# Layer 3's chunk norm in the output projection's place and one step earlier, and one state more for the producers in layer 1's finish and feed

## The chip, the core and the metric

The kernel runs on one core of a Trainium2 chip, as one program of four layers with the image data kept in HBM between them. The metric is the device time of one execution in microseconds; the runs shown are compared by their median. All arithmetic is float32. The engines are named as in the profile: PE (TensorE matmul), DVE (VectorE), ACT (ScalarE), POOL (GpSimd), and SP, which issues nearly all DMAs.

## The reference

Layers 1 and 3 are what the change touches. Both contain Mamba blocks, whose core is a scan over tokens for each of 16 states:

```
def step(h, inp):                       # layer 3; layer 1 is the same with other names
    dt_t, B_t, C_t, x_t = inp
    dA = jnp.exp(dt_t[:, :, None] * A)
    h = h * dA + (dt_t * x_t)[:, :, None] * B_t[:, None, :]
    y = jnp.einsum('bdn,bn->bd', h, C_t)
    return (h, y)
...
def rms_norm(x, w):
    return x * lax.rsqrt(jnp.mean(x * x, axis=-1, keepdims=True) + EPS) * w
def mamba1(x, ...):
    xn = rms_norm(x, nw)                # this is the "chunk's norm"
    ...                                 # projections, causal conv, scan, gate
    return y @ opw.T
...
xt = mamba_bidir(xt, P, 0, 1) @ tlin_w + tlin_b + xt    # "output projection" with the residual
xf = mamba_bidir(xf, P, 2, 3) @ flin_w + flin_b + xf
```

Layer 1, over 8 images of 64 x 64 pixels and 64 channels, scans in four directions, and then does, per image, a layer norm over 128 channels, a gate `y * silu(z)`, an output projection, a second norm, and a feed-forward part: a 1x1 and a depthwise 3x3 convolution, `gelu(h1) * h2`, and a 1x1 convolution.

## The kernel before, in words

**The scan stream.** `stream` (L462) drives layers 1 and 3. Work comes in steps of 1024 tokens-times-channels columns, and each step has 16 states, numbered n = 0 to 15 here; "3/8" will mean state 8 of step 3. A state i goes through a fixed pipeline: SP loads the rows of B and C (`fetch`), POOL or PE makes `hb` (the product with B: L526 on POOL, or `expand`, L2207, eight pieces of a product on PE, at states 1, 2, 5, 6, 9 and 10 of layer 3), ACT makes `dA` by an exponential (L520), DVE scans (L550), DVE or POOL multiplies by C (L564; POOL for the "shared" states), and PE adds the result up in PSUM (L310, L320). Every engine takes its instructions in the order in which the program issues them, so an instruction that waits holds up all that is queued behind it on its engine. The order is written by hand: nothing is reordered later.

**Tasks beside the scan.** All other work is cut into generators, "tasks", which are advanced by a piece at a time. `advance` (L437) is called once per state, before that state's scan is issued, and runs one piece. A piece ends at a `yield`: `yield True` means that the task holds the one PSUM buffer `mm` across the cut ("held"; the same task goes on until it lets go), `yield False` means that the next piece needs no PSUM, a bare `yield` means that the next piece wants PSUM and needs a "room". So a `yield` costs no instruction: it puts the following instructions one state later in the engines' queues.

**Layer 3.** It runs twice (s = 0, 1) over 16 chunks c of 2048 tokens: 32 chunks. A chunk has 8 steps (4 groups g of 512 tokens, forward and backward, k = 0, 1), so 128 states. Three things interleave with the scans:
- `prepare` of the step after next, by the fixed table `plan` (projection L2130, softplus, the six small diagonal DMAs `place` L2125 at states 3, 4, 5, 8, 9, 11, the gate).
- `begin`, the norm of the next chunk: eight DMAs `raw<-x` (L2044, 128 KB each, in pieces of 256 bytes); for each half j of the chunk a Square on ACT (L2053), the mean over channels on PE into `mm` (L310, `mm<-sq,mean`), a copy on ACT (L2058), a DMA to `rs` (L2060); then Sqrt (L2063), reciprocal on DVE (L2066), a DMA to HBM (L2069), eight broadcast DMAs `inv<-rs` (L2076, 256-byte pieces as well), and four multiplications `xn<-raw,inv` on POOL (L2083), `9` states apart.
- `finish`, the output projection of a group (L2246, L2249 on PE into `mm`, L2265 on ACT), which the end of every second step puts into the queue `urgent`.

`Step.rooms` names the states at which a piece that wants PSUM may run, `lets` the state at which a held `mm` is let go (ACT reads it, just before the scan of that state). Before the change, rooms are 7 and 11; `urgent` goes first and takes only 11; while `urgent` has a task that waits for its room, `behind` (the norm) does not move at all. `begin` of chunk c+1 is queued at the end of the first step of chunk c. `expand` of state 10 takes `mm` at state 7, after first releasing whatever holds it. `ready` forces the whole of a norm out before the first `prepare` that needs it (step 6, state 13).

**Layer 1.** Eight images, each 16 steps (4 directions, 4 pieces), so 256 states an image. While image b is scanned, the tasks of the image before run: `finish` (four times: POOL multiplies `inv` by z, L1162; PE applies `cent1`; DVE multiplies, L1167; projections; ACT copy), `begin` of image b+1, and `feed` (four times: three groups of convolution on PE; gelu on ACT, L1230; DVE multiplies, L1233; gelu, L1241; DVE multiplies, L1244). At state 2 of every step `begin_next` (inside `stream`) must hand `mm` to `prepare`, so it advances a held task until that task lets go, however many pieces that takes.

Of the kernel before, what the change touches and what calls it, by code (L numbers as in the profile page):

```python
# [16 lines left out]
NB = 8  # L17
# [255 lines left out]
class Net:  # L273
# [163 lines left out]
    def advance(self, behind, room=True, calm=True):  # L437


        while True:  # L440
            queue = self.held or (self.urgent if self.urgent else behind)
            if not queue or not (room or queue[0].said is False):
                return
            task = queue[0]
            if task.calm and not calm:
                return
            task.step()
            self.held = queue if task.said is True else None
            if not task.over:
                return  # L450
            queue.popleft()
# [10 lines left out]
    def stream(self, pools, ahead, steps, behind, rest=None):  # L462
# [115 lines left out]
        begun = {}  # L578
# [17 lines left out]
        for i in range(total + 2):  # L596
            at, n = divmod(i, NS)
            need(i + ahead[0], "bc")
            need(i + ahead[1], "du")
            fetch_c(i + ahead[2])  # L600
            fetch(i + ahead[0])
            multiply_b(i + ahead[1])
            if 0 < i <= total and shared(i - 1):
                multiply_c(i - 1)


            def begin_next():
                more = at + (2 if plan else 1)
                if more < len(steps) and n == steps[at].start:
                    steps[more].ready()  # L610
                    while self.held or self.urgent and not plan:
                        self.advance(behind)
                    return Task(steps[more].prepare())
                return work

            first = i > NS and n == 2
            if plan:
                before, behind_scan = plan.get(n, (0, 0))
                for _ in range(before if work else 0):
                    work.step()  # L620
                work = None if work and work.over else work
                if 2 < i <= total + 2 and shared(i - 3):
                    gather(i - 3)
                if 1 < i and not first and not shared(i - 2):
                    gather(i - 2)
                self.advance(behind, n in steps[0].rooms and not (n == 7 and self.urgent))
                if n in steps[0].lets and self.held:
                    self.release()
                if i < total:
                    scan(i)  # L630
                work = begin_next()
                for _ in range(behind_scan if work else 0):
                    work.step()
                if first:
                    gather(i - 2)
                if i < total and not shared(i):
                    multiply_c(i)
                if not direct(i + 2):
                    decay(i + 2)
                elif lent(i + 2):  # L640
                    expand(i + 2)
                if direct(i + 3):
                    decay(i + 3)
                    if not lent(i + 3):
                        expand(i + 3)
                continue
            late = i > 1 and not first and steps[0].late and shared(i - 2)
            if i > 1 and not late and not first:
                gather(i - 2)
            work = begin_next()  # L650
            if work is not None and not (self.held and work.said is None) and (calm(i) or not work.calm):
                work.step()
                if work.over:
                    work = None
            room = work is None or work.said is not True and (n < steps[0].early or hasattr(steps[at + 1], "du"))
            self.advance(behind, room, calm(i))
            if late:
                gather(i - 2)
            if i < total:
                scan(i)  # L660
            if first:
                gather(i - 2)
            if i < total:
                if not shared(i):
                    multiply_c(i)
            decay(i + 2)
# [292 lines left out]
    def layer1(self, src, dst):  # L959
        nc, tc, d = self.nc, self.tc, self.d  # L960
        mid = self.hbm["x1a"]
        with ExitStack() as ctx:
# [176 lines left out]
            def finish(b, chunks=range(4)):  # L1139

                q, rows = b // 2, slice((b % 2) * C, (b % 2) * C + C)
                hold = images[b]
                y = hold["y"]
                sums, again = hold.setdefault("sums", {}), hold.setdefault("again", {})

                def centred(c):
                    ps = pp.tile([128, T], F32, name="mm")
                    self.mm(ps, cent1, y[:, c * T : c * T + T])
                    yield True
                    return ps  # L1150

                yield from statistics(sums, centred, False, self.eps5, chunks)

                def output(c):
                    at = slice(c * T, c * T + T)
                    inv = spread(sums, c)
                    z = tp.tile([128, T], F32, name="tmp")
                    nc.sync.dma_start(z, hz[b, :, at])
                    x = tokens(src, b, c)
                    yield False  # L1160
                    yield
                    nc.gpsimd.tensor_tensor(inv, inv, z, ALU.mult)  # L1162
                    ps = pp.tile([128, T], F32, name="mm")
                    self.mm(ps, cent1, y[:, at])
                    yield True
                    yield True
                    nc.vector.tensor_tensor(inv, ps, inv, ALU.mult)  # L1167
                    yield
                    ps = pp.tile([128, T], F32, name="mm")
                    self.mm(ps, w_bias, z, start=True, stop=False)  # L1170
                    yield True
                    self.mm(ps, w_out, inv, start=False, stop=False)
                    self.sides(ps, self.ident2, x, start=False)
                    yield True
                    yield True
                    x = tp.tile([128, T], F32, name="tmp")
                    nc.scalar.copy(x, ps)
                    nc.scalar.dma_start(mid[q, rows, at], x[:C])
                    yield
                    ps = pp.tile([128, T], F32, name="mm")  # L1180
                    for r in range(2):
                        side, o = slice(r * C, r * C + C), slice(r * 512, r * 512 + 512)
                        nc.tensor.matmul(ps[:, o], centd[side], x[side, o], start=True, stop=True)
                    yield True
                    return ps

                yield from statistics(again, output, True, self.eps6, chunks)

            def feed(b, part=None):
# [37 lines left out]
                def gated(c):  # L1227
# [2 lines left out]
                    nc.scalar.activation(g, ps, AF.Gelu)  # L1230
                    yield
                    ps = yield from group(c, slice(128, 256))
                    nc.vector.tensor_tensor(g, ps, g, ALU.mult)  # L1233
                    yield
                    x = tokens(mid, b, c)
# [3 lines left out]
                    if c < 2 and part is None:  # L1239
                        fetch(c + 2)  # L1240
                    nc.scalar.activation(h, ps[:106], AF.Gelu)  # L1241
                    yield True
                    yield True
                    nc.vector.tensor_tensor(h[:42], ps[C : C + 42], h[:42], ALU.mult)  # L1244
# [36 lines left out]
            behind = deque()  # L1281
# [634 lines left out]
    def layer3(self, src, dst):  # L1916
# [8 lines left out]
        with ExitStack() as ctx:  # L1925
# [108 lines left out]
            def begin(s, c):  # L2034
# [5 lines left out]
                from_ = srcs[s][q, rows, part * 4 * W : (part + 1) * 4 * W].rearrange("p (s t) -> p s t", t=HW)  # L2040
                for g in range(4):
                    at = slice(g * H, g * H + H)
                    for r in range(2):
                        nc.sync.dma_start(x[r * C : r * C + C, at, ends[r]], from_[:, at])  # L2044
                        yield False
# [35 lines left out]
                for g in range(4):  # L2081
                    at = slice(g * H, g * H + H)
                    nc.gpsimd.tensor_tensor(hold["xn"][:, at], x[:, at], inv[:, at], ALU.mult)  # L2083

                    for _ in range(9 if g < 3 else 1):
                        yield False

            behind = deque()
            begun = {}
            images = {}  # L2090

            class Step:
                bc_shape, start = [128, 2, W], 13
                direct, lent, rooms, lets = fed, (1, 5, 9), (7, 11), (13,)
                plan = {
                    2: (0, 1), 3: (2, 0), 4: (1, 0), 5: (1, 0), 6: (0, 1), 7: (1, 0), 8: (1, 0), 9: (1, 0), 10: (0, 1), 11: (1, 0), 13: (0, 1), 15: (1, 0)
                }
# [132 lines left out]
                def done(self):  # L2230
                    hold = chunks[self.s, self.c]
                    if self.k == 1:
                        net.urgent.append(Task(finish(self.s, self.c, self.g, [hold["y0"], hold["y1"]])))
                    more = self.s * 2 * NB + self.c + 1
                    if self.k == 0 and self.g == 0 and more < 4 * NB:
                        at = divmod(more, 2 * NB)
                        begun[at] = Task(begin(*at))
                        behind.append(begun[at])

            def finish(s, c, g, ys):  # L2240
                w, dst = weights[s], dsts[s]
# [28 lines left out]
            with tc.manual_schedule():  # L2270
# [7 lines left out]
                steps = [  # L2278
                    Step(s, c, g, k) for s in range(2) for c in range(2 * NB) for g in range(4) for k in range(2)
                ]  # L2280
                self.stream(pools, (6, 3, 6), steps, behind)


# [24 lines left out]
```

## Time and profile before

| what | us |
|---|---|
| median of 3 runs (23713.9 to 23741.58) | 23733.38 |
| the profiled execution, device time | 23722.93 |
| its span, first to last instruction | 23721.1 |

The span by stage, from the trace's windows (busy us of each engine):

| stretch of the span, us | stage | length | PE | DVE | ACT | POOL | DMA share |
|---|---|---|---|---|---|---|---|
| 0 to 967 | layer 0, first norm of layer 1 | 967 | 739.14 | 448.44 | 459.95 | 57.76 | 0.34 |
| 967 to 8350 | layer 1 | 7383 | 6261.24 | 6673.97 | 3939.50 | 6781.89 | 0.89 |
| 8350 to 11247 | last feed-forward of layer 1, layer 2 | 2897 | 2452.07 | 2396.48 | 1370.19 | 2246.55 | 0.65 |
| 11247 to 23721 | layer 3 | 12474 | 10813.17 | 11850.59 | 9165.00 | 11492.05 | 0.62 |

Columns from PE on are busy time; an engine that is busy for nearly the whole length of a stretch bounds it. The mean granted clock of TensorE is 0.933. A row of the timeline, as shown in the prediction, reads: start, duration, engine, line, operation, tiles, how many instructions were merged, and in brackets the idle time of the engine before it with what ended the wait.

### The profile page before, as it was taken

Reading aid. Unit: us, or ns where it says so; the run is one execution under the profiler, and the core shown is the slowest. Engines: PE = TensorE matmul, PEld = TensorE weight load, DVE = VectorE, ACT = ScalarE, POOL = GpSimd, SP = SyncE. Lnnn points to the kernel's source line nnn. Section 1 sums busy time; section 2 is a strip of 40 time slices with the busy share of each in tenths; the row PEclk is TensorE's granted clock in tenths of the full one; section 3 lists DMA queues with packets and bytes.
Section 4 is the critical chain, followed back from the end, with each engine's and each line's share of the span. In section 5 each row is a group of like instructions: output and inputs, shape, how many; then the busy total and the mean of one; then the engine's idle time right before and its main releaser. Section 6 shows DMA issues by size and latency. Waiting matters only on the chain. (4 is left out here: it accounts for less than half of the span.)

```text
span 23721.1 us, 288888 instructions
## 1 busy us (share of the span) xinstructions
PE 20265.6 (85%) x99226; PEld 9428.8 (40%) x99226; DVE 21369.5 (90%) x12265; ACT 14934.6 (63%) x19503; POOL 20578.3 (87%) x9876
## 2 busy tenths in 40 slices
PE   7778888888888888879888888888888888888888
PEld 5323333333333323322444444444444444444444
DVE  5599999999999859977899999999999999999999
ACT  5445555555555446632677777777777777777776
POOL 0499999999999849986899999999999999999998
PEclk9889999999999999999899999999999999999999
DMA  3599889898898849961566666666666666666665
GB/s 80 190 325 322 309 313 320 312 318 317 310 317 312 287 148 340 342 212 35 171 184 185 179 183 184 182 183 182 184 183 184 183 185 183 184 181 184 182 182 172
DMA packets 2857344, 5295.40 MB, mean 223 GB/s; under 512 B 1357208, under 2 KB 1363452, under 8 KB 2853568
## 3 DMA queue, kind: packets, MB, share of 16 engines
q1 hardware_dynamic: 2831296, 5213.58, 68.9%
q10 hardware_dynamic: 24576, 63.33, 0.7%
q8 instruction: 785, 12.86, 0.2%
q14 instruction: 687, 5.63, 0.1%
HBM read 5112.98 MB, written 162.40 MB: 222 GB/s over the span
## 5 line engine op out<-in xcount | busy, mean ns | idle before, releaser
L526 POOL TENSOR_TENSOR hb<-du,bc 128x1024 f32<-128x1024 f32 x3072 | 7222.3, 2363 | 665.9 <-DVE h L550 301.5
L550 DVE TENSOR_TENSOR_SCAN dA<-dA,hb 128x1024 f32<-128x1024 f32 x2488 | 5675.5, 2281 | 189.4 <-POOL hb L526 105.7
L526 POOL TENSOR_TENSOR hb<-du,b 128x1024 f32<-128x1024 f32 x2048 | 4877.0, 2410 | 468.6 <-DVE dA L550 215.7
L564 POOL TENSOR_TENSOR h<-h,bc 128x1024 f32<-128x1024 f32 x2208 | 5175.8, 2359 | 106.1 <-DVE h L550 90.9
L520 ACT ACTIVATE dA<-dt,w_A 128x512 f32<-128x512 f32 x5120 | 3522.2, 689 | 1483.8 <-DVE hc L564 706.8
L520 ACT ACTIVATE dA<-dt,w_l_A 128x1024 f32<-128x1024 f32 x2560 | 2857.3, 1117 | 1006.1 <-DVE hc L564 765.3
L310 PE MATMUL acc<-hc,ident 128*128 128x512 f32 x7040 | 3387.3, 618 | 89.2 <-DVE img L1367 48.0
L550 DVE TENSOR_TENSOR_SCAN dA<-dA,carry,hb 128x1024 f32<-128x1024 f32 x1320 | 3093.1, 2343 | 120.9 <-POOL hb L526 59.0
L564 DVE TENSOR_TENSOR hc<-dA,bc 128x1024 f32<-128x1024 f32 x2400 | 2937.8, 1224 | 141.4 <-issue 2.7
L310 PE MATMUL acc<-h,ident 128*128 128x512 f32 x3200 | 1865.3, 712 | 880.4 <-POOL h L564 855.3
L320 PE MATMUL acc<-h,ident 64*64 64x512 f32 x16384 | 2156.7, 626 | 459.5 <-POOL h L564 458.7
L2207 PE MATMUL dA<-bc,duT 128*128 128x128 f32 x12288 | 1862.7, 314 | 546.6 <-ACT z L2183 518.3
L310 PEld LDWEIGHTS acc<-hc,ident 128*128 128x128 f32 x7040 | 1397.0, 202 | 2091.4 <-issue 1726.8
L2207 PEld LDWEIGHTS dA<-bc,duT 128*128 128x128 f32 x12288 | 1704.1, 222 | 1176.8 <-ACT z L2183 696.4
L320 PE MATMUL acc<-hc,ident 64*64 64x512 f32 x16384 | 2108.2, 608 | 0.0
L520 ACT ACTIVATE hb<-dt,w_A 128x512 f32<-128x512 f32 x3072 | 2038.7, 711 | 9.9
L550 DVE TENSOR_TENSOR_SCAN h<-hb,mm 128x1024 f32<-128x1024 f32 x768 | 1741.6, 2268 | 219.6 <-PE acc L320 179.0
L550 DVE TENSOR_TENSOR_SCAN h<-hb,dA 128x1024 f32<-128x1024 f32 x768 | 1752.0, 2281 | 189.4 <-PE dA L2207 157.3
L564 DVE TENSOR_TENSOR hc<-dA,c 128x1024 f32<-128x1024 f32 x1408 | 1722.7, 1224 | 118.1 <-DMA c<-bc 5.7
L550 DVE TENSOR_TENSOR_SCAN h<-dA,hb 128x1024 f32<-128x1024 f32 x712 | 1622.7, 2279 | 27.3 <-ACT dA L520 26.4
L2207 PE MATMUL mm<-bc,duT 128*128 128x128 f32 x12288 | 1603.8, 287 | 1.4 <-ACT u L2141 1.4
L2207 PEld LDWEIGHTS mm<-bc,duT 128*128 128x128 f32 x12288 | 1556.8, 205 | 3.3 <-ACT u L2141 2.2
(336 smaller groups left out, 26794.5 us busy)
## 6 DMA issues: line engine op xcount, KB each, us to landing
bc<-bc SPq DMA_DIRECT2D x2560, 512.0 KB
b<-bc SPq DMA_DIRECT2D x2048, 512.0 KB
c<-bc SPq DMA_DIRECT2D x2048, 512.0 KB
bc<-bc SPq DMA_DIRECT2D x512, 1024.0 KB
bc<-dg SPq DMA_DIRECT2D x1536, 256.0 KB
bc<-bc SPq DMA_DIRECT2D x1536, 256.0 KB
tmp<-rs SPq DMA_DIRECT2D x93, 512.0 KB
raw<-x SPq DMA_DIRECT2D x256, 128.0 KB
```

The costliest lines, as they stand in the source:

```text
L310: self.nc.tensor.matmul(o, lhsT, r, start=start, stop=stop)
L320: self.nc.tensor.matmul(acc[j * C : j * C + C, r * 512 : r * 512 + 512], lhsT(j)[at, at], rhs[at, j * 512 : j * 512 + 512], start=start, s ...
L520: nc.scalar.activation(o[:, cut], s.dt[:, cut], AF.Exp, scale=A[:, n : n + 1])
L526: nc.gpsimd.tensor_tensor(s.shaped(hb[i]), s.shaped(s.du), B.pop(i), ALU.mult)
L550: nc.vector.tensor_tensor_scan(h[:, way], dA[i][:, way], b[:, way], s.first(n), ALU.mult, ALU.add)
L564: engine.tensor_tensor(s.shaped(o), s.shaped(h), CC.pop(i), ALU.mult)
L2207: nc.tensor.matmul(hb[:, at], self.duT[:, at], diag[:, m * 128 : m * 128 + 128], start=True, stop=True)
```

## The change

In layer 3 `rooms` becomes the single state 11 (the norm's PSUM pieces take the place in a step that the output projection has), the norm of chunk c+2 is queued at the end of chunk c's last step (one step before the old place), a norm's pieces without PSUM may run while `urgent` waits for its room, the load of a chunk's last quarter waits until the old chunk's projection has been issued, and the four multiplications by `inv` stand 6 states apart. In layer 1 three `yield`s are added: after the POOL multiplication L1162, before the DVE multiplication L1233, and before the DVE multiplication L1244. No instruction is added or removed.

```diff
@@ advance
-            queue = self.held or (self.urgent if self.urgent else behind)
+            queue = self.held or self.urgent or behind
+            if not self.held and self.urgent and behind and not room and self.urgent[0].said is not False and behind[0].said is False:
+                queue = behind
@@ stream
-                self.advance(behind, n in steps[0].rooms and not (n == 7 and self.urgent))
+                self.advance(behind, n in steps[0].rooms)
@@ layer 1, finish
                     nc.gpsimd.tensor_tensor(inv, inv, z, ALU.mult)
+                    yield
                     ps = pp.tile([128, T], F32, name="mm")
@@ layer 1, feed
                     ps = yield from group(c, slice(128, 256))
+                    yield True
                     nc.vector.tensor_tensor(g, ps, g, ALU.mult)
...
                     nc.scalar.activation(h, ps[:106], AF.Gelu)
+                    yield True
                     yield True
                     yield True
                     nc.vector.tensor_tensor(h[:42], ps[C : C + 42], h[:42], ALU.mult)
@@ layer 3, begin
                 for g in range(4):
                     at = slice(g * H, g * H + H)
+                    while g == 3 and net.urgent:
+                        yield False
...
-                    for _ in range(9 if g < 3 else 1):
+                    for _ in range(6 if g < 3 else 1):
                         yield False
@@ layer 3
+            def start(s, c):
+                begun[s, c] = Task(begin(s, c))
+                begun[s, c].said = False
+                behind.append(begun[s, c])
...
-                direct, lent, rooms, lets = fed, (1, 5, 9), (7, 11), (13,)
+                direct, lent, rooms, lets = fed, (1, 5, 9), (11,), (13,)
@@ layer 3, Step.done
-                    more = self.s * 2 * NB + self.c + 1
-                    if self.k == 0 and self.g == 0 and more < 4 * NB:
-                        at = divmod(more, 2 * NB)
-                        begun[at] = Task(begin(*at))
-                        behind.append(begun[at])
+                    more = self.s * 2 * NB + self.c + 2
+                    if self.k == 1 and self.g == 3 and more < 4 * NB:
+                        start(*divmod(more, 2 * NB))
@@ before the stream of layer 3
+                start(0, 1)
                 self.stream(pools, (6, 3, 6), steps, behind)
```

## The prediction

> **What bounds it now.** I read the page's busy line, then its slices, then the windows by stage. The change touches layers 1 and 3 only.
>
> ```profile
> PE 20265.6 (85%) x99226; PEld 9428.8 (40%) x99226; DVE 21369.5 (90%) x12265; ACT 14934.6 (63%) x19503; POOL 20578.3 (87%) x9876
> DVE  5599999999999859977899999999999999999999
> POOL 0499999999999849986899999999999999999998
> ```
>
> In layer 3 DVE is busy 11850.59 of 12474 us, POOL 11492.05. The starts of DVE's scans (L550) in the timeline give every state's length. A step has 16 scans of 2.28 us, 8 products of 1.22 and a drain of 1.2: in the timeline they follow each other with no gap over most of a step, and an undisturbed step takes 47.5 us. The mean of the 31 chunks that carry a norm is 387.1 us, against 8 x 47.5 = 380: some 7 us a chunk, 218 us in all, is what better placing can reach. By step (0 to 7) the means are 48.2, 47.5, 47.9, 49.9, 49.6, 47.8, 48.8, 47.5. In layer 1 an image takes 917 us, POOL is busy 849 of them and DVE 836: POOL leads, DVE is close.
>
> **Layer 3, step 3: the norm's first half.** The timeline of the sixth chunk, states 8 to 10:
>
> ```profile
> 13430.88 2.62 PE L310 MATMUL mm<-sq,mean 64*1 64x512 f32 x4 [1.72 <-ACT z L2183]
> 13433.43 3.78 PE L2207 MATMUL dA<-bc,duT 128*128 128x128 f32 x16
> 13433.59 1.00 ACT L2058 COPY sq<-mm 1x1024 f32<-1x1024 f32 x1
> 13434.61 0.52 SPq L2060 DMA_DIRECT2D rs<-sq  x1
> 13437.32 2.29 DVE L550 TENSOR_TENSOR_SCAN h<-hb,dA 128x1024 f32<-128x1024 f32 x1 [2.39 <-PE dA L2207]
> 13437.39 1.08 ACT L2053 ACTIVATE sq<-raw 64x1024 f32<-64x1024 f32 x1 [2.80 <-DMA rs<-sq]
> 13440.95 2.29 DVE L550 TENSOR_TENSOR_SCAN h<-hb,mm 128x1024 f32<-128x1024 f32 x1 [1.35 <-PE acc L320]
> ```
>
> The mean's products stand on PE in front of the expansions for states 9 and 10, so DVE waits 2.39; the next Square stands on ACT behind a DMA just issued. States 8 and 9 together last 9.04 us here, and 6.67 in the mean of the other steps. The change moves the products to state 11 of step 1, the copy to 13. The second half does exactly this in step 3 now, and states 11 to 15 of step 3 show no loss. So 2.37 x 31 = **-74 us**. What is late next is the usual wait at state 9 (0.6 to 1 us in every step), which stays. The second Square now stands in step 1, state 15, behind its DMA: by the same DMA of step 3 (issued 1.9 us into state 15; 2.8 us to landing) it has landed before ACT gets there. Its 1.07 us push the exponentials for state 2, which now end 1.2 us before their scan: +0.1 us a chunk at most. The first Square goes from 2/0 to 1/1, the same phase, and cost nothing there.
>
> **Layer 3, steps 5 to 7: the four multiplications (1.40 us each) on POOL.** Now the first goes out at 5/12 and the rest at once at 6/13, forced by `ready`:
>
> ```profile
> 14376.32 4.13 POOL L2083 TENSOR_TENSOR xn<-raw,inv 128x560 f32<-128x560 f32 x3
> ...
> 14417.59 1.99 PE L320 MATMUL acc<-h,ident 64*64 64x512 f32 x8 [3.52 <-POOL h L564]
> ...
> 14429.12 2.29 DVE L550 TENSOR_TENSOR_SCAN h<-hb,dA 128x1024 f32<-128x1024 f32 x1 [0.98 <-ACT hb L520]
> ```
>
> POOL has 2.6 us to spare in a step (47.5 less 10 + 8 products of 2.36 and one of 2.4), so 4.13 at once leave it late through all of step 7: PE waits for L564, then the expansion for state 1 is late (the row names ACT, which had long been done; PE's expansion ended 0.1 us before). States 0 and 1 last 6.55 us in step 0, 7.16 in step 6, and 5.77 in quiet steps: 0.78 and 1.39 us. By the built order the four now go to 5/4, 5/10, 6/0 and 6/6. At 5/4, 6/0 and 6/6 POOL's own gaps follow (0.7, 0.8, 0.6 at states 2 to 4; 0.2 and 1.15 at 8 and 9) and take them up. At 5/10 none follows until state 2: everything for the next step is 1.4 us late. Here a rule speaks against the change: the Trainium skill ("TensorE: Matmul & The Clock Gate", section "Why this matters for your kernels") wants no idle gap of PE over about 3 us, lest its clock fall by half. PE's gap there is about 1.3 us; 1.3 + 1.4 = 2.7 stays under the rule: slack 0.8 us, cost 0.6 x 31 = 19 us. The row says less room: in the trace groups after gaps of 2.5 us and more often run at half speed (1.99 against 1.09 us above), and the seven chunks whose step 7 is late by 1.35 to 1.6 us lose 0.87. I take the row: 27 us. So step 6 gains (1.39 - 0.87) x 31 = **-16**, and step 0 (0.78 less the 0.15 that step 1, also without PE work at 11, loses now) x 31 = **-20**.
>
> **Layer 3, SP.** An issue takes 0.6 us alone, and up to 6.8 where one of the six `place` DMAs falls into the same state:
>
> ```profile
> L2044 SPq DMA_DIRECT2D raw<-x x256: 585/635/5205, 11247.1 to 23027.4; - x128
> L2076 SPq DMA_DIRECT2D inv<-rs x256: 579/1962/6824, 11279.6 to 23213.8; - x128
> ```
>
> (minimum/median/maximum ns.) Behind them the loads of B and C wait, then POOL. `inv` moves from 5/2..5/9, with five `place`, to 4/7..4/10 and 4/14..5/1, with two: better, and the phase in which `raw` stands now at no visible loss. `raw` takes the bad phase, 0/3 to 0/8, with four. In step 5 that delayed POOL by 0.95 us in the mean, 3.1 at worst; beyond 0.9 it reaches DVE, which gives 0.43 us by the same chunks. Ends: 0 and 1.3; I take 0.4 x 31 = **+12**. Step 2's loss of 0.15, from `raw` at 1/7, goes: -4; step 5 and the second Square give +3. The row DMA moves from 4/14 to 4/3, where SP has no backlog: nothing. Sqrt and reciprocal stay at 4/0 to 4/2, with their 2.3 us. Layer 3: -74 - 16 - 20 + 12 - 4 + 3 = **-99 us**.
>
> **Layer 1.** What the yields are to remove, in images 2 to 7 (1837 to 7340 us), from the waits:
>
> ```profile
> DVE tmp L1244 <- ACT tmp L1241: 64.0, 12, 5.4
> DVE tmp L1233 <- PE mm L1025: 62.7, 24, 6.2
> DVE tmp L1167 <- POOL tmp L1162: 32.9, 21, 2.9
> ```
>
> Twelve waits of 5.4 us, and six of the 24 with 6.2, are at state 2 of a step, where `begin_next` runs a held task to its end; another `yield True` there only lengthens that loop. The rest, about 59 us, is DVE waiting while POOL is busy or itself waits for a DMA (L1162 <- hz: 13.4 us): the time between such a wait and the next POOL product shows POOL idle only at 2/2, 2/3, 14/0 and 14/2. I count 2.8 us an image, not 10.
>
> Against it: shifted by a state here and there, pieces fall under the loop of state 2. Stepping through both orders, it runs 13 pieces an image now and 26 afterwards (four of them empty). The price, from two drains of the fourth image:
>
> ```profile
> 4252.18 2.83 PE L1025 MATMUL mm<-strip,hright 64*106 64x512 f32 x12
> 4255.05 1.02 ACT L1241 ACTIVATE tmp<-mm 106x1024 f32<-106x1024 f32 x1 [1.70 <-PE mm L1025]
> 4256.11 1.23 DVE L1244 TENSOR_TENSOR tmp<-mm,tmp 42x1024 f32<-42x1024 f32 x1 [5.30 <-ACT tmp L1241]
> ...
> 4317.86 1.23 DVE L1233 TENSOR_TENSOR tmp<-mm,tmp 128x1024 f32<-128x1024 f32 x1 [6.21 <-PE mm L1025]
> ```
>
> At 10/2 and 13/2 the convolution's right taps, until now issued a state earlier, join the drain. The drain at 11/2 already has them and waits 6.21 without the gelu; with the gelu's 1.02 and its hops that is 7.5 against 5.3: +2.2 each, 4.4. At 5/2 three quarters of the statistics of `begin` come at once: a chain of three copies and two Squares on ACT (1.0 each) and four PE groups (1.0 to 1.1) is about 11 us in front of an exponential; DVE has some 6 us of work meanwhile (scans, products, the drain L1367) and POOL one product more in hand: +3. At 3/2 and 4/2 projections join: +1.3. At 6/2 and 12/2: +0.8. Sum 9.5 - 2.8 = 6.7 an image, x6 = 40; the last image, with 24 drained pieces for 15, +6. Layer 1: **+46 us**, between 0 and 225 (below).
>
> **The sum.** The profiled execution took 23722.9 us: 23722.9 - 99 + 46 = 23670. The median of the runs is 10.4 higher; halving that, I predict **23675 us**.
>
> **Rivals.**
> - *Layer 1 is free*: POOL's buffers cover the longer drains, as they cover part of the present ones (DVE waits 6.2, POOL 4 to 5). 23733 - 99 = 23634, or some 20 lower if the step-0 loads cost nothing. Against it: POOL is already empty at 10/2 and 13/2. Chance 0.20.
> - *Layer 3 gives half back*: every chunk's `raw` in step 0 behaves like the worst `inv` chunks of step 5 (2 us late at DVE): +50 more, so -49 + 46: 23730. For it: the phase is the same. Against it: four collisions, not five, and the output projection keeps PE busy at 0/11. Chance 0.18.
> - *Slower*: each drained piece costs what one costs now. Around the drains of layer 1 POOL idles some 33 us an image for 13 pieces, 2.5 us each. 13 more: 33 x 6 + 25 = 225 against 99: 23733 + 126 = 23859. It decides from 1.1 us a piece on (87 pieces against 99 us). Against it: the empty pieces and the last piece of a chain cost nothing. Chance 0.13.
> - That the change doesn't do what it says is excluded by the built order.
>
> **The numbers.** Forecast 0.49, its own range 23625 to 23720. A measurement here tells 0.2%, 47 us, from no change. Faster by more: 0.34 of the forecast and the 0.20 of free drains, 0.54. Same: 0.15 of the forecast, 0.16 of the half-back case, 0.31. Slower: 0.15. The range from 23590 to 23760 leaves out the slower rival and the tail of the free one.
>
> **What would show it.** States 8 and 9 of step 3 as in other steps, no `rs<-sq` wait before L2053 (70.7 us in 29 now); states 0 and 1: about 5.9 us in step 0, 6.6 in step 6, 6.2 in step 1; `inv` issues mostly at 0.6 us; the wait of L1167 gone while the image stays at 917 us or grows to 924. It would be wrong if layer 3's chunks don't come down to about 384 us, or if an image of layer 1 moves by over 10 us.

## The result, and the profile after

| what | before | after |
|---|---|---|
| median of 20 runs each, us | 23717.79 (23706.0 to 23745.29) | 23757.04 (23733.22 to 23784.75) |
| ratio of after to before, 95% interval | | 1.0016, [1.0009, 1.0023] |
| span of the profiled execution, us | 23721.1 | 23744.8 |

The change makes the kernel slower, by about 39 us. Forecast was 23675, faster by over 0.2% as the likeliest case; 23757 is at the upper edge of the stated range, on the wrong side of before. The sign is clear of noise, the size is just under 0.2%.

The page of after, busy time and slices:

```profile
PE 20169.9 (85%) x99226; PEld 9371.3 (39%) x99226; DVE 21371.1 (90%) x12265; ACT 14940.4 (63%) x19503; POOL 20575.2 (87%) x9876
...
DVE  5598988988989949988799999999999999999999
...
POOL 0499989999999939986799999999999999999999
```

The instruction counts are those of before and so is the busy time of DVE and POOL, within some 3 us: all of the difference is waiting. The slices show where most of it lies: in the first half, where layer 1 is, digits of DVE have fallen from 9 to 8; in the second half, layer 3, they show next to nothing. The starts of DVE's scans give it in us. (State n of step k, written k/n, is here the time from that scan's start to the next. Lines of kernel.py are shifted by a few from kernel to kernel: the scan is L550 before and L552 after.)

| from the starts of the scans, us | before | after | difference |
|---|---|---|---|
| layer 1, 2048 scans | 7754.7 | 7828.5 | +73.8 |
| an image of it (mean of images 1 to 6) | 917.2 | 929.6 | +12.4 |
| layer 3, first to last scan | 12379.9 | 12333.8 | -46.1 |
| a chunk of it (mean of 31) | 387.06 | 385.66 | -1.40 |

The forecast had +46 for layer 1 and -99 for layer 3. Both signs are right and both sizes are wrong, and each error goes the same way. By step (0 to 7), the chunks of layer 3 moved by -5, +11, **+31**, -69, -35, +13, **+9** and +1 us in all (mean difference by 31), where the forecast had -8 for step 0, 0, -4, -74, 0, +3, -16 and 0.

### The profile page after: what moved, and what is told of

Read it like the earlier page. It is cut to its first block, busy times and chain, and to the rows that moved or that the text cites. A ratio compares the mean times of both kernels' runs of the same rounds, so it can differ in the third digit from the quotient of the medians.

```text
span 23744.8 us, 289011 instructions
## 1 busy us (share of the span) xinstructions
PE 20169.9 (85%) x99226; PEld 9371.3 (39%) x99226; DVE 21371.1 (90%) x12265; ACT 14940.4 (63%) x19503; POOL 20575.2 (87%) x9876
## 5 line engine op out<-in xcount | busy, mean ns | idle before, releaser
L552 DVE TENSOR_TENSOR_SCAN dA<-dA,hb 128x1024 f32<-128x1024 f32 x2488 | 5675.6, 2281 | 185.0 <-POOL hb L528 116.8
L566 POOL TENSOR_TENSOR h<-h,bc 128x1024 f32<-128x1024 f32 x2208 | 5179.3, 2360 | 110.8 <-DVE h L552 105.6
L522 ACT ACTIVATE dA<-dt,w_A 128x512 f32<-128x512 f32 x5120 | 3521.3, 689 | 1515.4 <-DVE hc L566 718.8
L522 ACT ACTIVATE dA<-dt,w_l_A 128x1024 f32<-128x1024 f32 x2560 | 2857.4, 1117 | 1007.7 <-DVE hc L566 760.7
L552 DVE TENSOR_TENSOR_SCAN dA<-dA,carry,hb 128x1024 f32<-128x1024 f32 x1320 | 3094.2, 2344 | 148.0 <-POOL hb L528 79.6
L566 DVE TENSOR_TENSOR hc<-dA,bc 128x1024 f32<-128x1024 f32 x2400 | 2937.8, 1224 | 141.0 <-issue 2.7
L522 ACT ACTIVATE hb<-dt,w_A 128x512 f32<-128x512 f32 x3072 | 2039.1, 711 | 10.7
L552 DVE TENSOR_TENSOR_SCAN h<-hb,mm 128x1024 f32<-128x1024 f32 x768 | 1742.1, 2268 | 214.6 <-PE acc L320 151.1
L552 DVE TENSOR_TENSOR_SCAN h<-hb,dA 128x1024 f32<-128x1024 f32 x768 | 1752.2, 2281 | 135.7 <-PE dA L2219 73.5
L566 DVE TENSOR_TENSOR hc<-dA,c 128x1024 f32<-128x1024 f32 x1408 | 1722.8, 1224 | 124.8 <-DMA c<-bc 12.2
L552 DVE TENSOR_TENSOR_SCAN h<-dA,hb 128x1024 f32<-128x1024 f32 x712 | 1622.7, 2279 | 47.2 <-ACT dA L522 40.0
L566 POOL TENSOR_TENSOR h<-h,c 128x1024 f32<-128x1024 f32 x640 | 1518.4, 2373 | 19.4 <-ACT carry L1355 19.0
```

The source lines that it names most:

```text
L522: nc.scalar.activation(o[:, cut], s.dt[:, cut], AF.Exp, scale=A[:, n : n + 1])
L552: nc.vector.tensor_tensor_scan(h[:, way], dA[i][:, way], b[:, way], s.first(n), ALU.mult, ALU.add)
L566: engine.tensor_tensor(s.shaped(o), s.shaped(h), CC.pop(i), ALU.mult)
```

## Where the time went, in the trace of after

**Layer 1, from the scan of 5/2 to that of 5/4.** It took 9.6 us an image before and takes 24.7 now. The timeline of after, fourth image:

```profile
3985.73 1.02 PE L1052 MATMUL mm<-tmp,mean 64*1 64x512 f32 x4
3986.80 1.00 ACT L1057 COPY tmp<-mm 1x1024 f32<-1x1024 f32 x1 [0.72 <-PE mm L1052]
...
3990.13 1.54 PE L1052 MATMUL mm<-tmp,mean 64*1 64x512 f32 x4 [1.15 <-ACT tmp L1047]
...
3995.99 1.87 PE L1052 MATMUL mm<-tmp,mean 64*1 64x512 f32 x4 [1.15 <-ACT tmp L1047]
3997.91 1.00 ACT L1057 COPY tmp<-mm 1x1024 f32<-1x1024 f32 x1 [1.97 <-PE mm L1052]
...
3998.97 3.68 PE L310 MATMUL mm<-u,w_l_xp 128*68 128x512 f32 x4 [1.10 <-ACT tmp L1057]
...
3999.68 1.12 ACT L522 ACTIVATE dA<-dt,w_l_A 128x1024 f32<-128x1024 f32 x1
...
4004.12 1.28 ACT L1062 ACT_TABLE_LOAD   x1 [0.43 <-ACT dbl L1329]
...
4005.77 0.35 DVE L1064 RECIPROCAL rs<-rs 128x32 f32<-128x32 f32 x1 [12.89 <-ACT carry L1355]
...
4006.03 2.25 DVE L552 TENSOR_TENSOR_SCAN h<-dA,carry,hb 128x1024 f32<-128x1024 f32 x1
```

The drain (the pieces that `begin_next` forces out at state 2 of a step) runs the norm's statistics as one chain, PE, ACT, PE, ACT, each link waiting for the one before. It begins with the copy at 3986.80, and the exponential (L522) stands behind it at 3999.68, 12.9 us later. But that is not what DVE waits for last. The exponential ends at 4000.80, and the scan starts at 4006.03: it stands behind the norm's reciprocal, which waits for the Sqrt (L1062; the row blames the `carry` copy that precedes it on ACT), which stands on ACT behind the copy of a projection that took PE 3.68 us. DVE sits idle for 12.89 us, POOL for 14.27.

**Layer 3, 2/0 and 2/1: the second Square.** The timeline of after, fifth chunk (`SPq` rows are issues):

```profile
13028.62 1.00 ACT L2065 COPY sq<-mm 1x1024 f32<-1x1024 f32 x1
...
13030.05 0.37 SPq L2232 DMA_DIRECT2D bc<-bc  x1
...
13033.73 4.66 POOL L566 TENSOR_TENSOR h<-h,bc 128x1024 f32<-128x1024 f32 x2
...
13036.11 0.32 SPq L2232 DMA_DIRECT2D bc<-bc  x1
13036.53 0.54 SPq L2067 DMA_DIRECT2D rs<-sq  x1
...
13040.61 1.08 ACT L2060 ACTIVATE sq<-raw 64x1024 f32<-64x1024 f32 x1 [2.38 <-DMA rs<-sq]
...
13042.99 1.33 ACT L522 ACTIVATE hb<-dt,w_A 128x512 f32<-128x512 f32 x2
...
13044.41 2.29 DVE L552 TENSOR_TENSOR_SCAN h<-hb,mm 128x1024 f32<-128x1024 f32 x1 [1.95 <-ACT hb L522]
```

The copy ends at 13029.62, but its row DMA is issued at 13036.53. Ahead of it on SP stand two loads of B and C (L2232). Each is issued in under 0.4 us, but the second waits 5.6 us for the first of the two POOL multiplications (L566). Such a wait stands in state 15 of step 3 too, before and after: it is the order of the program, and no slowness of the load. The row DMA lands 4.1 us after its issue. ACT comes to the Square 2.38 us before that, and the exponential for the next state, queued behind, makes DVE wait 1.95. This chunk is one of the worse ones. In the median of 30 chunks the row DMA goes out 2.5 us after the scan of 1/15; where the Square waits for it (26 times) it takes 3.6 us to land in the median, and the least is 3.1. The waits of layer 3, before and after:

```profile
DVE h L550 <- PE dA L2207: 157.3, 189, 2.7
...
DVE h L550 <- ACT hb L520: 23.9, 14, 4.8
```

```profile
DVE h L552 <- ACT hb L522: 79.2, 53, 4.0
DVE h L552 <- PE dA L2219: 73.5, 163, 2.1
...
ACT sq L2060 <- DMA rs<-sq: 29.1, 26, 2.9
```

(total us, times, longest.) By the scan that waits, the 84 us that DVE no longer waits for PE's expansions are mostly three things: 3/9 (63.6 before, 4.4 now) and 4/5 (27.7, 6.7), which are most of the gain of steps 3 and 4, and 6/1, where the wait only has another name: 24.3 for PE and 11.1 for ACT before, 49.7 for ACT (26 times) in after. The second Square's own share of the 79.2 is the wait at 2/2, 20.3 us in 22 times, where before had none. The Square's wait for its DMA fell from 70.7 us to 29.1, and did not go.

## Experiments

Each is compared with runs of the kernel before on the same chip.

**The two parts apart.** First the change of layer 3 alone, that is after without layer 1's three yields:

```diff
-                    yield            # behind L1164, z
-                    yield True       # ahead of L1237
-                    yield True       # ahead of L1249
```

> The change of layer 3 alone: layer 1 is as before. Theory (the two parts of the change are independent, and the profile after gives each its size): layer 3's scans take 46 us less as in the profile after, so about 23672 us, ratio 0.9981, and an image of layer 1 is back at 917 us. Rival 1 (the prediction's own size for layer 3): 99 us less, ratio 0.9958. Rival 2 (layer 3's smaller gain is an effect of layer 1's part on it): layer 3 comes down by clearly more than 46 us here.

Measured: ratio 0.999 [0.9984, 0.9997], 23700.55 against 23724.27 us. The scans of layer 1 take 7741.2 us, so its part is undone; those of layer 3 take 12364.8, 15 us less than before and not 46. Steps 2 and 1 are 21 and 10 us worse than in after, the others agree within 8. Whether the Square's wait varies that much from execution to execution, or layer 1 has a part in it, one profile of each kernel does not tell. Rival 1 is dead, and so is rival 2: layer 1 did not hide a larger gain. The theory's own 0.9981 lies just outside the interval as well: the change of layer 3 by itself is worth about 24 us by the medians, not 46.

Then layer 1's yields in the kernel before, the one in `finish` and the two in `feed` separately:

> Before, with only the new yield behind the product of the statistics with z (first of layer 1's three). Built order: it alone puts five pieces (the rest of a norm's statistics) into the drain at step 5, state 2. Theory: step 5 grows by 15 to 17 us an image, steps 2 to 4 give back 5 to 6, the convolution's drains (steps 10, 13) do not change: about +70 us, ratio 1.003. Rival (the prediction's prices: 3 us at step 5, 2.1 at steps 3, 4, 6, less 2.8 gained): about +15 us, ratio 1.0006.

> Before, with only the two new yields of the feed-forward (behind the second group and behind the last Gelu). Built order: the drains at steps 10 and 13 have six pieces instead of four, step 11 five, step 5 none, as before. Theory (from the profile after): steps 10 and 13 lose about 2 us each and steps 9 and 12 give back 2 to 3 each: within 10 us of before, ratio 1.000. Rival (the prediction's prices: 4.4 us an image lost and nothing gained): +27 us, ratio 1.0011.

Measured: the yield in `finish` alone 1.0033 [1.0021, 1.0045], the two in `feed` 1.0 [0.9992, 1.0008]. In the first, 5/2 and 5/3 together go from 9.6 to 24.0 us, steps 2 to 4 give 5.3 back, and steps 8 to 15 are as before (459.2 and 459.0 us); in the second 10/1 and 13/1, where DVE waits for the longer drains, go from 8.9 and 9.0 to 10.8 and 11.1, and steps 9 and 12 give 4.2 back. Both theories hold, and the prediction's prices (1.0006 and 1.0011) lie outside the intervals. One yield carries layer 1's whole loss. The waits in images 2 to 7, before and in its run:

```profile
DVE rs L1062 <- ACT carry L1350: 18.4, 10, 2.3
```

```profile
DVE rs L1062 <- ACT carry L1351: 72.1, 8, 11.5
...
DVE tmp L1168 <- POOL tmp L1162: 5.1, 4, 2.0
```

The last row is the wait that the yield was to remove: 32.9 us before, 5.1 now. The first is what came for it: DVE's wait for the norm's reciprocal.

**Is it the yield, or what falls into the drain?** The same yield, with one empty piece taken out two lines below:

```diff
                     nc.gpsimd.tensor_tensor(inv, inv, z, ALU.mult)
+                    yield
                     ps = pp.tile([128, T], F32, name="mm")
                     self.mm(ps, cent1, y[:, at])
                     yield True
-                    yield True
                     nc.vector.tensor_tensor(inv, ps, inv, ALU.mult)
```

> Before, with the new yield behind the product of the statistics with z, and one of the two empty pieces behind the following matmuls taken out, so that a chain has as many pieces as before and only these matmuls come a state later. Built order: the drain at step 5, state 2 is empty again, the others have as many pieces as before. Theory (what costs is the norm's statistics in the drain of step 5, not the yield itself): an image of layer 1 is back at 917 us within 3 us, ratio 1.000. Rival (the matmuls' later place itself costs): slower by 20 us or more.

Measured: 1.0002 [0.9993, 1.0011]; an image takes 915.4 us, 5/2 and 5/3 9.6, and the wait for the reciprocal is 15.7 us. So the later place of the matmuls is harmless (the interval alone would leave room for 26 us, the trace does not); the piece more per chain, which pushes the statistics of the next norm under the drain of 5/2, is what costs. Nothing is gained either: DVE's wait at L1167 is now mostly for PE (36.7 us, and 13.4 for POOL).

**The second Square, two states later:**

```diff
                     nc.sync.dma_start(rs[j * 64 : j * 64 + 64], ...)
+                    if j == 0:
+                        yield False
+                        yield False
```

> The change of layer 3 alone, with two more empty pieces ahead of the second Square, so that it stands at state 1 of step 2 instead of state 15 of step 1. Theory (in the profile after, this Square waits on ScalarE for the row DMA issued just ahead of it, whose issue is late on SP, and the exponential for state 1 of step 2 stands behind it): the Square's wait goes and state 1 of step 2 falls from 3.0 to 2.2 us, 25 us in all against the change of layer 3 alone, ratio about 0.997. Rival (something else is late at state 1 of step 2, as the expansion or POOL): no difference to the change of layer 3 alone, 0.9981.

Measured: 0.9967 [0.9954, 0.9979], 23644.58 us, where the same without this edit, in the same session, took 23700.55. 2/1 is 2.22 us (3.32 in the run of layer 3 alone) and all of step 2 falls by 1.95 us a chunk, 60 us. The timeline of this run, fifth chunk:

```profile
12959.25 0.54 SPq L2064 DMA_DIRECT2D rs<-sq  x1
...
12963.22 2.28 DVE L552 TENSOR_TENSOR_SCAN h<-hb,dA 128x1024 f32<-128x1024 f32 x1
...
12964.28 1.06 ACT L2057 ACTIVATE sq<-raw 64x1024 f32<-64x1024 f32 x1
```

The Square starts 5.0 us after the row DMA's issue, with no wait, and the scan in front has none either. DVE's waits for that exponential in all of layer 3 fall to:

```profile
DVE h L552 <- ACT hb L522: 56.4, 30, 4.3
```

The theory has the place right. The edit gained twice the 25 us that were expected: step 2 had lost 52 us in this build's own base, and 31 in after.

**The four multiplications on POOL.** On top of the later Square:

```diff
-                yield False
-                yield False
                 hold["xn"] = p2.tile([128, 4 * H, HW + 6], F32, name="xn")
...
-                    for _ in range(6 if g < 3 else 1):
+                    for _ in range((6, 10, 6, 1)[g]):
                         yield False
```

> The change of layer 3 with the second Square at state 1 of step 2, and the four multiplications on POOL at 5/2, 5/8, 6/2 and 6/8 instead of 5/4, 5/10, 6/0 and 6/6 (step/state). Theory (POOL's gaps lie at states 2 to 4 and 8 to 9 of every step, and a multiplication ahead of them is taken up): states 14 of step 5 and 0 of step 6 lose 0.9 us a chunk less, up to 28 us against the run with the later Square. Rival (step 5 is late because of the inv loads on SP, wherever the multiplications stand): no change, or slower since the first multiplication then waits for inv.

Measured: **0.9947 [0.9935, 0.996]**, 23571.39 against 23696.71 us; layer 3's scans take 12242.3 us, 72 less than with the later Square alone. By the two ratios (0.9967 and 0.9947, on different chips) it is some 47 us, and their intervals just overlap. 6/0 goes from 5.20 to 3.83 us and 5/14 from 2.43 to 2.20: that is 50 us of the 72, where the theory had up to 28. How 5/10 differs from 5/8 is seen in the fourteenth chunk, after first:

```profile
16698.92 1.40 POOL L2090 TENSOR_TENSOR xn<-raw,inv 128x560 f32<-128x560 f32 x1
16699.01 1.98 PE L320 MATMUL acc<-h,ident 64*64 64x512 f32 x8 [3.02 <-POOL h L566]
...
16704.90 4.65 POOL L528 TENSOR_TENSOR hb<-du,bc 128x1024 f32<-128x1024 f32 x2
...
16704.98 1.98 PE L320 MATMUL acc<-h,ident 64*64 64x512 f32 x8 [3.99 <-POOL h L566]
...
16707.27 2.30 DVE L552 TENSOR_TENSOR_SCAN dA<-dA,hb 128x1024 f32<-128x1024 f32 x1 [2.04 <-POOL hb L528]
...
16712.34 1.26 ACT L2153 ACTIVATE u<-mm,w_cb 128x512 f32<-128x512 f32 x2 [3.11 <-PE mm L2142]
...
16716.27 2.29 DVE L552 TENSOR_TENSOR_SCAN h<-hb,dA 128x1024 f32<-128x1024 f32 x1 [1.92 <-ACT hb L522]
```

and the version with 5/2 and 5/8 at the same place:

```profile
16578.56 4.67 POOL L528 TENSOR_TENSOR hb<-du,bc 128x1024 f32<-128x1024 f32 x2
...
16578.65 1.98 PE L320 MATMUL acc<-h,ident 64*64 64x512 f32 x8 [3.28 <-POOL h L566]
...
16581.32 2.28 DVE L552 TENSOR_TENSOR_SCAN h<-dA,hb 128x1024 f32<-128x1024 f32 x1
...
16590.48 2.28 DVE L552 TENSOR_TENSOR_SCAN h<-hb,dA 128x1024 f32<-128x1024 f32 x1
```

In after POOL starts the multiplication of 5/10 at state 12, being late already, and finds no pause before it delivers `hb` for state 15: DVE waits for it, 2.04 us. PE is late with it, a projection (L2142) is late behind PE's groups, ACT waits 3.11 for the projection, and the exponential for 6/1 is queued behind: DVE waits once more, 1.92. In the other version both waits are gone, though PE's groups after a long gap still run at about half speed (1.98 us where others take 1.09). Over layer 3 the wait for the exponential, of which 49.7 us stood at 6/1 in after and 47.4 with the later Square, is down to 3.4 there, and in all to:

```profile
DVE h L552 <- ACT hb L522: 15.7, 11, 4.1
```

**The last loads of `raw`, and `inv`.** Two attempts to remove what is left at 1/0 and 5/0 (0.3 to 0.5 us each):

```diff
                 for g in range(4):
                     at = slice(g * H, g * H + H)
-                    while g == 3 and net.urgent:
-                        yield False
                     for r in range(2):
                         nc.sync.dma_start(x[r * C : r * C + C, at, ends[r]], from_[:, at])
                         yield False
+                while net.urgent:
+                    yield False
+                for _ in range(2):
+                    yield False
```

The second run has this edit too, and besides the multiplications of the last run and the later half of the `inv` loads moved into step 5.

> The change of layer 3 with the second Square at state 1 of step 2, and with the wait for the output projection put behind the last two loads of raw: all eight go out at states 3 to 10 of step 0, none at 14 and 15. Theory (on SP the two loads stand ahead of the loads of the diagonals that the expansion for state 1 of step 1 waits for): state 0 of step 1 falls from 4.0 to 3.6 us, 10 to 14 us in all against the run with the later Square; step 0 does not change. Rival (the prediction's: the phase of states 3 to 8 of step 0 is the bad one): state 0 of step 1 stays, and steps 0 and 1 lose more.

> The change of layer 3 with all three: the second Square at state 1 of step 2, raw at states 3 to 10 of step 0, the multiplications at 5/2, 5/8, 6/2, 6/8, and besides only four inv loads in step 4, the other four at 5/3 to 5/6 instead of 4/14 to 5/1. Theory: state 0 of step 5 falls by the 0.5 us that inv ahead of the diagonals costs; 35 to 55 us less than with the later Square alone, ratio 0.995. Rival: the inv loads at 5/3 to 5/6 delay the loads of B and C there, and the gain of step 5 is gone: ratio 0.997.

In both the residual of a chunk's last group is taken from the rows of the chunk after next, so neither computes the model's result: the wait that this edit moves is what keeps the loads behind the old chunk's last output projection. Measured: 1.0021 [1.0011, 1.003] and 1.0008 [0.9999, 1.0017]. The loss is one new wait at 0/13, 5.3 us a chunk:

```profile
16402.28 1.94 PE L2258 MATMUL mm<-raw,w_res 64*64 64x512 f32 x2 [3.81 <-DMA raw<-x]
...
16410.93 2.29 DVE L552 TENSOR_TENSOR_SCAN h<-dA,hb 128x1024 f32<-128x1024 f32 x1 [5.42 <-ACT out L2277]
```

The projection's product (`raw,w_res`) now waits for the loads just issued. 1/0 fell to 3.6 us, but a stall of 5 us ahead of it lets every other engine catch up, so this tells nothing of the loads. The `inv` half can be read: with no `inv` at 4/14 to 5/1 state 5/0 stays at 4.1 us, as with them. That theory falls, as far as a kernel with that stall in step 0 can tell. For `raw` the question was put again without the side effect, the last quarter being loaded behind the first Square, on top of the best version:

```diff
                     nc.scalar.activation(o, x[:C, j * 2 * H : (j + 1) * 2 * H, ends[0]], AF.Square)
+                    if j == 0:
+                        yield False
+                        yield from load(3)
                     yield
```

(`load(g)` is the loop body of before; the first three quarters go out as they did.)

> The version with the later Square and the multiplications at 5/2, 5/8, 6/2 and 6/8, with the last two loads of raw at states 2 and 3 of step 1 (behind the first Square, which does not read them) instead of 14 and 15 of step 0; the wait for the output projection stays ahead of them. Theory (at 14 and 15 they stand on SP ahead of the loads of the diagonals for state 1): state 0 of step 1 falls from 3.9 to 3.6 us and nothing else moves: 10 us less than without this edit, ratio 0.994. Rival (states 2 and 3 have no room on SP either): the loss moves to states 1 to 5 of step 1, ratio 0.9947 or more.

Measured: 0.9943 [0.993, 0.9957], not to be told from the 0.9947 without it; 1/0 is 3.92 us where it was 3.87. The two loads at 0/14 and 0/15 are not what costs there. What does was not found. The scan that waits there (1/1 and 5/1) waits mostly for PE's expansion, 5.6 and 11.6 us in after; both follow loads of 256-byte pieces in the states before, as the prediction had it. Half of them out of step 4 changed nothing at 5/0, and no run takes all away.

## Why the prediction was wrong

Both signs that it named for being wrong came: layer 3's chunks came down to 385.7 us and not to about 384, and an image of layer 1 moved by over 10 us.

- **What bounds the kernel, the step-3 gain**: right. 2.37 us a chunk were expected from taking the mean's products away from 3/8 and 3/9; these states went from 9.04 to 6.81 us, -69 in all for step 3 against -74.
- **"+0.1 us a chunk at most" for the second Square**: the first of four terms that were wrong. The prediction took issue and landing from the DMA of the other half (1.9 us into state 15, 2.8 us to landing). In the median of after it is 2.5 and 3.6: 1.4 us later in all, where the exponential's margin of 1.2 us was already taken up by the Square's own 1.07. Where SP is held longer, as in the chunk shown, it is 3.8 and 4.1. Step 2 lost 31 us in after and 52 in layer 3 alone; two empty pieces remove 60.
- **The multiplication at 5/10**: second. "1.4 us late, slack 0.8, cost 0.87" left step 6 a gain of 16 us. It lost 9, and step 5 lost 13 where, together with the Square, 3 were forecast. The rule of the clock and the row of half-speed groups were weighed for PE, but POOL was late before: in the chunk shown it did not get to the second multiplication until state 12. The prediction saw itself that "at 5/10 none follows" and did not draw the end of it: the new spacing, with the multiplications at 5/2, 5/8, 6/2 and 6/8, is worth 72 us by the traces.
- **"At 5/2 three quarters of the statistics ... +3"**: third, and the largest. The chain in front of the exponential was put at 11 us, and DVE's work meanwhile at 6. Both were near: from the first copy to the exponential it is 12.9 in the image shown, 11.0 to 11.6 in the run with this yield alone, where the loss is nearly the same, and DVE works on for 6.1 us. What the sum left out is the exponential's own 1.1, 2.3 to 2.6 us in which DVE's drain (L1372) waits for PE, and above all 5.2 from the end of the exponential to the scan: the reciprocal on DVE, behind the Sqrt, follows the drained pieces and now stood ahead of that scan. It cost 15.1 us an image, 91 over six, for 18.
- **"I count 2.8 us an image, not 10"** for what the yields gain: fourth, and it hid part of the third. The prediction put DVE's waits while POOL is busy at next to nothing. But steps 2 to 4 gave 5.3 us an image in the run of the first yield, steps 9 and 12 gave 4.2 in that of the other two: nearly all of the 59 us of waits came back as time.
- **The other drains.** +2.2 each was forecast for 10/2 and 13/2, and 1.9 and 2.1 were measured (at 10/1 and 13/1); 3/1, 6/1 and 12/1 cost 2.6, 1.2 and 1.1, where 2.1 stood for them and 4/2 together. So an image has +15.1, +4.0 and +4.9, less 11.6 given back, +12.4; the forecast was 3 + 4.4 + 2.1 - 2.8 = 6.7. The last image's +6 did not show (-0.7).
- **Step 4's 35 us** were a gain that no term had, and without it layer 3 would have gained 11 us: this was luck. Its states 4 and 9 fell by 0.61 and 0.51 us. In the sixth chunk the expansions for 4/9 and 4/10 took 2.72 and 2.93 us before and 2.02 and 1.95 after; why they were slow before was not tried.
- **`raw` in step 0, +12, and 0/0, -20**: near in sum. Steps 0 and 1 together moved by +6, for -8; 0/0 went from 4.19 to 3.69, and 1/0 from 3.57 to 3.80, as said above without a cause. `inv` issues came down as forecast, from a median of 1.96 us to 0.61, but `raw` issues in the "bad phase" have a median of 0.63, as before.
- **The slower rival** had the right place and a wrong law. It priced each drained piece alike; those that `feed` added cost 4.0 us an image and were given back, those at 5/2 cost 15, so it was decided by which pieces join a drain, and not by how many. Of what was to show it: the wait of L1167 for POOL went, as said, and the image grew beyond the 924 us that bounded the forecast.

Together: layer 3 gave 53 us less than forecast (35 the Square, 35 the multiplications, 13 steps 0 and 1, 5 step 3, less 35 gained in step 4), and layer 1 cost 28 more.

The best version found is the change of layer 3 without layer 1's yields, with the Square two states later and the multiplications at 5/2, 5/8, 6/2 and 6/8: 0.9947 of before, 125 us less.

## What to carry to other kernels

A drain that runs a queued task to its end is priced by the chain that falls into it, every instruction of it: also the small one on the bounding engine at its far end. A wait of one nearly full engine is not worthless because another nearly full one is busy meanwhile: here it came back almost whole. Before moving an instruction behind a DMA, look up what the issuing queue waits for in that state, and take the spread of that DMA's time and not one value: it was 1.9 to 3.5 us at 3/8 of before, and 3.1 to 4.3 at the new place. An extra operation on an engine that is nearly full belongs ahead of a gap of that engine; two states decided, in the chunk shown, whether two waits of about 2 us came or not.

## What was not expected of the hardware

The clock of PE can be halved without a long gap. In the chain of 5/2 above the granted clock is 0.50 from 3991 to 4004, and the same small group (L1052) takes 1.87 us at 3995.99 where it took 1.02 at 3985.73, though no idle time of PE between is longer than 1.15 us. So the length of the gaps alone, as the prediction weighed it, does not tell when it happens; what does was not tried. Nor was it expected that a change of order alone would lower PE's busy time by 96 us (20265.6 to 20169.9) at equal counts. It is layer 3: there PE's busy time falls from 10813 to 10709 us, and its granted clock rises from 0.94 to 0.95, while the kernel as a whole became slower.
